# Mamba stage: the product with the old state in halves of the rows, one product for the decays' row sums, one set of eight PSUM banks, and new offsets for the order

## The chip, the cores and the metric

The kernel runs on one core of a Trainium2 chip, in float32 throughout. The time is the device time of one execution in microseconds; the kernel's time is the median over its runs. A core has TensorE (PE, a 128 x 128 array of multipliers that reads its stationary operand by weight loads, PEld, and streams the moving operand past it), VectorE (DVE), ScalarE (ACT), GpSimd (POOL) and SyncE (SP, which here only issues transfers). The results of PE land in PSUM, which holds eight banks of 128 partitions x 512 floats.

## The reference

The input x is an image batch of 2 x 256 x 48 x 48. Layer 0 is a local attention (7 x 7) with a convolution branch. Layer 1 treats the image as 2 x 2304 tokens of 256 features: a Mamba block and then eight experts of which each token takes two. What matters here is the Mamba block's scan, with 8 heads of 64 features and a state of 64:

```python
xn = _rmsnorm(x, norm_w, eps)
zxbcdt = jnp.einsum('bld,ed->ble', xn, W_in)          # z, x, B, C, dt
...
dt = jax.nn.softplus(dt + dt_bias)
dA = jnp.exp(dt * -jnp.exp(A_log))
def step(state, inp):
    dA_t, dt_t, B_t, C_t, x_t = inp
    state = state * dA_t[:, :, None, None] + (dt_t[:, :, None] * x_t)[..., None] * B_t[:, None, None, :]
    y = jnp.einsum('bhpn,bn->bhp', state, C_t)
    return (state, y)
...
y = jnp.moveaxis(ys, 0, 1) + Dp[None, None, :, None] * xs
y = _rmsnorm(y * jax.nn.silu(z), gnorm_w, 1e-05)
return x + jnp.einsum('ble,de->bld', y, W_out)
```

Behind it stand a layer norm, the gating (`xf @ Wg`, the two largest of eight) and the experts (`gelu(xf @ W1[e]) @ W2[e]`, weighted and summed).

## The kernel before

**Three stages.** Layer 0 runs to about 321 us of the span, the Mamba block from there to about 789 us, and the experts to the end at 1294 us. In the last fifth of the Mamba stage PE also works on the first three tiles of one expert ("early" tiles, lines 1805 and 1821), chosen once 24 of the 36 chunks have been gated.

**The scan in chunks.** The 4608 tokens are cut into 36 chunks of 128 (`chunk`, number c), of which three (NJ) make a block of 384 (TB; number k). 18 chunks belong to each image, so two chunks (`fresh`) start from no state and 34 start from the state that the chunk before left. Instead of one step per token, a chunk is computed by products of matrices:

- `pst` (line 1371) forms what the chunk adds to the state: the turned B times the decayed inputs xw. The state is a tile of 128 x 256: heads 0 to 3 on partitions 0 to 63, heads 4 to 7 on partitions 64 to 127, with the 64 state dimensions along the partitions of each half. This product writes its two halves of PE's columns and is marked `mode="tiled"`. POOL multiplies the old state by the chunk's decay (`decayed`, L1397), and DVE adds the two (`state`, L1420).
- `ps` (`from_state`, L1390) is the old state's part of the output: state times C, for all 128 tokens. It makes four matmuls, one for every 128 of the 512 features, with 128 columns of the state as the stationary operand. Since the partitions hold two groups of heads, each matmul takes all 128 rows and the moving operand cz is a tile [128, 2, 384] that holds C twice: in part 0 on the upper 64 partitions with zeros below, in part 1 the other way round. The zeros are written once; two transfers per block (`ct`) copy C in from the tile bc, which has B on partitions 0 to 63 and C on 64 to 127. The result fills one PSUM bank; DVE multiplies it by the tokens' decays rd (`yi`, L1410, one instruction of 128 x 512), and POOL adds that to y (`yb`, L1425).
- `py` (L1433) is the part from within the chunk: eight matmuls into halves of the columns (`mode="tiled"`), of xd and a matrix mt of 128 x 8 x 128 that ACT (`al`, `mt`, L1345 and L1359) and DVE (`mm`, L1353) make from the sums of the decays.
- y goes through `ya` (DVE, L1441), `yz` (POOL, L1443), `sq` (ACT), `sm` (POOL, L1458), `ss` (PE, L1461), `rs` (DVE), `rg` (POOL, L1497), and the product with W_out, `out` (PE, L1451), whose result is added into the residual.

POOL's part of a chunk stands in the lines xw (L1317), dx (L1332), `decayed`, `yb`, `yz`, `sm`, `rg`, and then in the scatters of the gating.

**The decays of a block.** `decays_of` holds `su`, the sums along the chunk, and `er` (`starts`, L1220): for each of the three chunks one matmul with the 8 columns of a as the stationary operand and a triangle of ones as the moving one, so that the results lie as [8 heads, 3 x 128 tokens]. ACT copies them out of the bank twice, once with an exponential, into the tile `from` [8, 2, 384]; the transfer `spread` lays them out in memory as (kind, chunk, head, token), from where `rd` and `row` read them back, spread over partitions.

**Gating.** The chunks are gated in seven groups (6, 6, 6, 6, 6, 4, 2). A group begins when its last chunk's residual is done, forms counts on PE (`g6`, L1609), and ends in two indirect transfers per chunk that POOL issues (`put`, L1679), which scatter the rows to the experts' table. The experts can start when the last of them have landed.

**What sets the order.** Within the Mamba stage all of this is laid out by a list planner (`Flow`). Every operation has an engine, a cost in ns, needs, and slots that it takes and gives back (`room`: six PSUM banks named bank, two named zbank for the projections of the gates z, two cz, three bc, and so on). An operation's rank is its due time (its chunk's number times `PACE1`, 16387 ns), less the rest of its own chain, less an offset per kind of operation (`LEAD1`, 95 numbers). The planner plays the engines' times by these costs; of the operations that are ready and have their slots it emits the one with the lowest rank, with a surcharge where PE would change its mode. The order that it emits is PE's, DVE's, ACT's and SP's order in the program, instruction by instruction, and POOL's is held by explicit order edges. The costs and offsets exist only in the planning: on the chip an instruction starts when its engine has come to it and the tiles it reads and writes are free.

Of the kernel before, what the change touches and what calls it, by code (L numbers as in the profile page):

```python
# [31 lines left out]
F32 = mybir.dt.float32  # L32
# [196 lines left out]
class Kernel:  # L229
# [688 lines left out]
    def mamba(self, ctx):  # L918

        nc = self.nc
        self.ps = self.pool("ps", 1, space=bass.MemoryType.PSUM)
        self.used_banks = ["zbank0", "zbank1"]

        room = dict(bank=6, zbank=2, cvbank=2, t=3, xn=2, xc=2, bc=3, cz=2, z=2, btt=2, xd=3, xw=2,
                    mt=4, yi=1, y=4, sq=2, state=3, rd=2, u2=2, ex=1, ext=1, ehid=2, ey=2)
        self.begin_flow(self.pool("m", 1, ctx), room, self.PACE1, self.LEAD1)
        zeros = self.pool("cz", 1, ctx)
        self.cz = [zeros.tile([P, 2, TB], F32, name=f"cz{i}") for i in range(room["cz"])]  # L930
        for t in self.cz:
            nc.gpsimd.memset(t, 0.0)
        for k in range(B * NBLK):
            self.norms(k)
            self.project_block(k)
            self.decays_of(k)
            for c in range(k * NJ, (k + 1) * NJ):
                self.chunk(c)
        first = 0
        for g, n in enumerate(GROUPS):  # L940
            self.gate(g, first, n)
            first += n
        self.adds = {}
        self.early_expert(sum(GROUPS[: EARLY + 1]))
        for i in range(NEARLY):
            self.early_tile(i, sum(GROUPS[: EARLY + 1]))
        self.run_flow()
# [3 lines left out]
        "al": -290978, "begin": 28518, "btt": 903929, "ct": -258969, "cum": 138318, "cv": 4160,  # L951
        "decayed": 600184, "dg": 29752, "dt": 100727, "dx": -4156, "ea": -277213, "ebegin":
        -102059, "ed": -105474, "efetch": 1438, "eg": 26883, "eown": 41250, "eplan": -216891,
        "eput": -260074, "er": 287202, "es": -882262, "et": -610518, "etoken": -82312, "eu":
        -375317, "ew": 321735, "eweight": -249839, "ex": -22495, "ext": 45975, "from": 77621,
        "g10": -530705, "g5": 86017, "g6": 266930, "g8": 619114, "g9": -284332, "ge": -53696,
        "gm": -98648, "gmrs": 207272, "grs": 157083, "gsm": -121187, "gsw": -603090, "gw":
        -597259, "head": -444384, "kap": 244339, "keep": -167944, "lg": -74165, "mm": 175579,
        "mo": -45640, "mrs": 201963, "msw": -491777, "mt": -64622, "n2": -327525, "nt": 132852,
        "number": -110107, "out": -69798, "pg": -24798, "place": 60192, "ps": 382782, "pst":  # L960
        95326, "put": -322183, "py": 88837, "rd": 122406, "rg": -214014, "row": 58828, "rs":
        216632, "rs1": -164526, "s0": 477684, "s4": 611494, "s5": 133846, "scores": -252255,
        "silu": -226005, "silub": 88047, "silux": 101715, "sm": 481060, "spread": -243362, "sq":
        -69048, "sr": -36881, "ss": -35615, "st": -60640, "state": -249719, "stats": -437860,
        "su": -1199, "tap": 131999, "tb": 14763, "tc": 292305, "tx": 467979, "u2": -251857,
        "xc": 488195, "xd": 18280, "xo": 475933, "xt": 66896, "xw": 407174, "ya": 7940, "yb":
        -85276, "yi": -88374, "yz": -140873, "z": -15500,
# [228 lines left out]
    def decays_of(self, k):  # L1196
# [20 lines left out]
        def starts():  # L1217
            ps = self.bank_for(("er", k))
            for j in range(NJ):
                nc.tensor.matmul(  # L1220
                    ps[:SH, j * P : (j + 1) * P], lhsT=T["a", k][:, j, :], rhs=self.c["le"], start=True, stop=True
                )

        def rows_of(i, func):
            nc.scalar.activation(T["from", k][:, i, :], T["bank", ("er", k)][:SH, :TB], func)

        def spread():
            to = self.decays[k].rearrange("i j s t -> s i j t")
            nc.sync.dma_start(to, T["from", k].rearrange("s i (j t) -> s i j t", j=NJ))
# [8 lines left out]
        op("er", "PE", 660, starts, ("s5", k), takes=[("bank", ("er", k))])  # L1238
        self.chain(k * NJ, ("from", k), [
            ("ACT", 480, lambda: nc.scalar.copy(  # L1240
                self.small_tile("from", k, [SH, 2, TB], bufs=2)[:, 1, :], T["bank", ("er", k)][:SH, :TB])),
            ("ACT", 480, lambda: rows_of(0, AF.Exp)),
# [8 lines left out]
        for i in range(NZ):  # L1251
            at = (k, i)

            def gate(i=i, at=at):
                if i == 0:
                    self.large_tile("z", k, [P, NZ, TB])
                T["zbank", at] = self.next_bank([f"zbank{self.flow.slot['zbank', at]}"], "zbank")
                self.project(
                    T["zbank", at][:, :TB], lambda h: win[:, h, i * P : (i + 1) * P], lambda h: T["xn", k][:, h, 3:]
                )  # L1260

            op(("z", at), "PE", 1300, gate, *rows, ("z", (k, i - 1)) if i else None,
               takes=[("zbank", at)] + ([("z", k)] if i == 0 else []), uses=[("xn", k)])

        taps = [("tap", ((k, m), 2)) for m in range(NM)]
        for i in range(NZ):
# [5 lines left out]
               uses=[("zbank", at)], chain=(("silu", k), i < NZ - 1))  # L1272
# [5 lines left out]
        def ct():  # L1278
            nc.sync.dma_start(self.cz[k % len(self.cz)][:DS, 0, :], T["bc", k][DS:P, :])
            nc.sync.dma_start(self.cz[k % len(self.cz)][DS:, 1, :], T["bc", k][DS:P, :])  # L1280
# [9 lines left out]
    def chunk(self, c):  # L1290
# [56 lines left out]
        def pg():  # L1347
            nc.tensor.matmul(
                self.bank_for(("pg", c))[:, :P], lhsT=T["bc", k][:, cols], rhs=cz[:, 0, cols], start=True, stop=True
            )  # L1350
# [34 lines left out]
        else:  # L1385
            def from_state():
                ps, old = self.bank_for(("ps", c)), T["state", c - 1]
                for m in range(NZ):
                    g, i = divmod(m, 2)
                    nc.tensor.matmul(  # L1390
                        ps[:, m * P : (m + 1) * P], lhsT=old[:, i * P : (i + 1) * P], rhs=cz[:, g, cols],
                        start=True, stop=True,
                    )
# [15 lines left out]
            def yi():  # L1409
                nc.vector.tensor_tensor(  # L1410
                    self.large_tile("yi", c, [P, NZ, P]), self.parts(T["bank", ("ps", c)]), T["rd", c], ALU.mult
                )

            op("rd", "queue", 2800, rd, ("spread", k), takes=[("rd", c)])
            op("ps", "PE", 900, from_state, ("state", c - 1), ("ct", k), ("rd", c), takes=[("bank", ("ps", c))],
               uses=[("state", c - 1)] + ([("cz", k)] if last else []))
# [7 lines left out]
            op("yi", "DVE", 690, yi, ("ps", c), ("rd", c), takes=[("yi", c)], uses=[("bank", ("ps", c)), ("rd", c)])  # L1424
# [941 lines left out]
```

## Time and profile before

| | us |
|---|---|
| median of three runs | 1292.45 (1290.72 to 1294.8) |
| the profiled execution's own time | 1295.8 |
| its span, from the first to the last instruction | 1294.0 |
| stages: layer 0 / Mamba / experts | 321.7 / 467.5 / 504.9 |
| busy in the Mamba stage: PE, DVE, ACT, POOL | 445.8, 356.7, 367.4, 372.7 |
| product with the old state, L1390, 272 records of PE | 36.4 busy |
| yi, L1410, 34 instructions on DVE | 23.3 busy |
| mean granted clock of TensorE | 0.986 |

Lines such as L1390 are lines of the kernel; in the groups of instructions `bank<-cz,state` names the tile written and the tiles read. A float32 matmul stands in the records as two passes, so the 272 records of L1390 are 34 products of four matmuls. The records of neighbouring matmuls overlap, and the sum of their busy times is more than the time that PE gave them; where a price of PE is wanted, it is taken from start to start. PE is busy for 95% of the span, DVE 71%, ACT 61%, POOL 43%; but over the Mamba stage POOL has 372.7 us of 467.5, and its share is uneven.

### The profile page before, as it was taken

To read this page: it belongs to the slowest core of one execution; us is meant where nothing else is said; L and a number is where in the kernel's file an instruction comes from. 1 tells how busy PE (TensorE), PEld (TensorE's weight loads), DVE (VectorE), ACT (ScalarE), POOL (GpSimd) and SP (SyncE) were. 2 spreads that over 40 slices of the span, in tenths; PEclk is the share of its full clock that TensorE was granted. 3 is DMA by queue.
4 is the path that set the end of the run, shared out by engine and by line. 5 is a ranking of instruction groups with operands and counts; after the bars stand their busy time and mean duration, and the time that the engine had idled before them with its cause. 6 is when DMAs were issued, how large, how long until landed. Compare 5 with 4: busy or idle time off the path is not lost. (4 is left out here: it accounts for less than half of the span.)

```text
span 1294.0 us, 23558 instructions
## 1 busy us (share of the span) xinstructions
PE 1232.5 (95%) x8048; PEld 983.4 (76%) x8048; DVE 924.8 (71%) x2425; ACT 792.7 (61%) x1954; POOL 557.6 (43%) x769
## 2 busy tenths in 40 slices
PE   4999999998799999999999997999999999999995
PEld 3566766665567777777777786999999999999994
DVE  5899999999577887879797745555654665566442
ACT  2598978898799888789697552333333333333342
POOL 4411230210357878999889963212121212221220
PEclk9999999999799999999999998999999999999998
DMA  7331322211132234333636238657667667666756
GB/s 283 126 104 41 100 92 76 80 49 41 43 107 89 91 116 120 116 114 120 187 117 186 64 133 278 184 169 254 203 221 236 192 198 228 235 188 199 233 178 208
DMA packets 101658, 194.12 MB, mean 150 GB/s; under 512 B 10635, under 2 KB 82652, under 8 KB 96604
## 3 DMA queue, kind: packets, MB, share of 16 engines
q1 hardware_dynamic: 85020, 168.51, 38.3%
q0 software_dynamic: 14400, 19.74, 7.8%
q10 hardware_dynamic: 2116, 4.33, 1.0%
q8 instruction: 66, 1.08, 0.3%
q14 instruction: 56, 0.46, 0.1%
HBM read 154.24 MB, written 43.23 MB: 153 GB/s over the span
## 5 line engine op out<-in xcount | busy, mean ns | idle before, releaser
L2095 POOL DMA_INDIRECT acc<-ey,token x70 | 108.7, 1552 | 368.5 <-ACT ey L2094 312.1
L2085 PE MATMUL bank<-ext,wt 128*128 128x256 f32 (+1 forms) x1152 | 241.3, 368 | 0.0
L2089 ACT ACTIVATE hid<-bank,bt 128x256 f32<-128x256 f32 (+1 forms) x288 | 132.3, 461 | 170.7 <-PE bank L2085 166.5
L2085 PEld LDWEIGHTS bank<-ext,wt 128*128 128x128 f32 x1152 | 207.0, 190 | 25.0
L681 POOL COPY kp<-kp 128x10 f32<-128x10 f32 (+1 forms) x60 | 24.9, 415 | 179.4 <-DVE kp L674 179.4
L592 DVE SCALAR_TENSOR_TENSOR x<-hid,w2r,x 128x1128 f32<-128x1128 f32 (+3 forms) x72 | 99.9, 1392 | 0.4 <-ACT hid L586 0.2
L2128 PE MATMUL po<-ts,ss 128*128 128x128 f32 x768 | 96.2, 275 | 0.0
L916 PE MATMUL bank<-xn,win 128*128 128x387 f32 x240 | 92.7, 510 | 2.1 <-ACT t L999 2.1
L1129 DVE SCALAR_TENSOR_TENSOR xc<-bank,vec,xc 128x384 f32<-128x384 f32 x144 | 86.6, 610 | 8.4 <-ACT xc L1118 8.1
L2128 PEld LDWEIGHTS po<-ts,ss 128*128 128x128 f32 x768 | 90.9, 192 | 0.0
L1345 ACT ACTIVATE mt<-mt,cum 128x128 f32<-128x128 f32 x288 | 87.8, 393 | 1.7 <-DMA mt<-decays 1.7
L800 ACT ACTIVATE prob<-prob,top 128x308 f32<-128x308 f32 x144 | 78.3, 552 | 16.0 <-DVE top L789 15.6
L1679 POOL DMA_INDIRECT xs<-u,rows x72 | 72.9, 1012 | 17.4 <-issue 14.7
L2132 ACT COPY u<-po 128x128 f32<-128x128 f32 x32 | 8.5, 266 | 114.2 <-PE po L2128 114.2
L2072 DVE TENSOR_TENSOR ss<-hid 128x512 f32<-128x512 f32 x32 | 22.1, 691 | 70.6 <-ACT hid L2089 70.6
L1451 PE MATMUL bank<-wout,y 128*128 128x264 f32 x288 | 72.0, 396 | 0.1
L916 PE MATMUL zbank<-xn,win 128*128 128x384 f32 x192 | 71.2, 492 | 0.5 <-ACT z L1247 0.3
L806 ACT ACTIVATE prob<-prob,rden 128x308 f32<-128x308 f32 x144 | 67.7, 550 | 3.7 <-DVE rden L855 3.7
L582 DVE SCALAR_TENSOR_TENSOR hid<-xp,vec,hid 128x1175 f32<-128x1175 f32 (+1 forms) x48 | 68.4, 1425 | 0.1
L2128 PE MATMUL po<-wt,hid 128*128 128x128 f32 x496 | 65.5, 275 | 0.0
L789 DVE CUSTOM_DVE_ANT_0 prob<-banks,cst 128x308 f32<-128x308 f32 x144 | 61.7, 471 | 3.9 <-PE banks L779 3.6
L916 PEld LDWEIGHTS bank<-xn,win 128*128 128x128 f32 x240 | 42.5, 195 | 24.8 <-issue 3.9
(334 smaller groups left out, 2989.6 us busy)
## 6 DMA issues: line engine op xcount, KB each, us to landing
wt<-in_We SPq DMA_DIRECT2D x36, 2048.0 KB
mt<-decays SPq DMA_DIRECT2D x36, 512.0 KB
ex<-xs SPq DMA_DIRECT2D x36, 265.0 KB
rd<-decays SPq DMA_DIRECT2D x68, 128.0 KB
val<-vtab SPq DMA_DIRECT2D x72, 110.0 KB
bt<-in_We SPq DMA_DIRECT2D x36, 136.0 KB
vraster<-vout SPq DMA_DIRECT2D x18, 256.0 KB
acc<-x SPq DMA_DIRECT2D x36, 128.0 KB
```

The source lines that it names most:

```text
L582: nc.vector.scalar_tensor_tensor(dst, src, w[:, k : k + 1], dst, ALU.mult, ALU.add)
L592: nc.vector.scalar_tensor_tensor(dst, src, w[:, k : k + 1], dst, ALU.mult, ALU.add)
L800: nc.scalar.activation(t, t, AF.Exp, bias=T["top", c][:, a : a + 1], scale=-1.0, accum_out=T["den", c][:, a : a + 1])
L916: self.nc.tensor.matmul(ps, lhsT=lhs(k), rhs=rhs(k), start=k == 0, stop=k == NH - 1)
L1129: nc.vector.scalar_tensor_tensor(out(), T["bank", ("cv", at)][:, i : i + TB], wc[:, i : i + 1], out(), ALU.mult, ALU.add)
L1345: nc.scalar.activation(t, t, AF.Relu, bias=at_s, scale=-1.0)
L1451: nc.tensor.matmul(ps[:, : C + E], lhsT=T["y", c][:, m, :], rhs=self.l1["wout"][:, m, :], start=m == 0, stop=m == NZ - 1,)
L1679: ins = nc.gpsimd.indirect_dma_start(self.xs, bass.IndirectOffsetOnAxis(ap=of("rows")[:, i, q : q + 1], axis=0), T["u2", g][:, i, :], None,)
L2085: nc.tensor.matmul(ps[:, :rows], lhsT=w1[:, k, c * P : (c + 1) * P], rhs=xt[:, k, :], start=k == 0, stop=k == NH - 1,)
L2089: nc.scalar.activation(hid[:, c, :], ps[:, :rows], AF.Gelu, bias=bt[:, c : c + 1])
L2095: put = nc.gpsimd.indirect_dma_start(self.acc, bass.IndirectOffsetOnAxis(ap=token[:, j : j + 1], axis=0), y, None, compute_op=ALU.add)
L2128: nc.tensor.matmul(p[name], lhsT=v[a][:, c], rhs=v[w][:, c], start=c == 0, stop=c == NHC // 2 - 1)
```

## The change

Five edits, all in the Mamba stage.

1. `ps` in halves of the rows: each of its four matmuls takes 64 partitions of the state and the 64 partitions of C that lie on the same rows (cz for the upper half, bc itself for the lower). The two groups of heads write to two banks, ps0 and ps1, of which each uses 256 columns. The operation is marked `mode="rows"` for the planner. `yi` becomes two instructions of 128 x 256, one for each bank.
2. cz is a tile [128, 384] without the second part, so `ct` is one transfer for two, and the tile is half as large to zero. bc is held until the block's last `ps`.
3. `er` is one matmul for the three chunks: its stationary operand is 24 columns of a, the result [24, 128]. The tile `from` becomes [24, 2, 128], and `spread` writes the same layout in memory from it.
4. The PSUM banks: eight named bank, of which the gates' projections take theirs too. zbank remains as a counter (three) with no memory of its own.
5. The planner's costs follow (`ps` 900 to 460, `er` 660 to 224, `yi` 690 to 800, the copies of `from` 480 to 280), and all 95 offsets are replaced, so the order of the whole stage is new.

```diff
-        self.used_banks = ["zbank0", "zbank1"]
+        self.used_banks = []
-        room = dict(bank=6, zbank=2, cvbank=2, t=3, xn=2, xc=2, bc=3, cz=2, z=2, btt=2, xd=3, xw=2,
+        room = dict(bank=8, zbank=3, cvbank=2, t=3, xn=2, xc=2, bc=3, cz=2, z=2, btt=2, xd=3, xw=2,
                     mt=4, yi=1, y=4, sq=2, state=3, rd=2, u2=2, ex=1, ext=1, ehid=2, ey=2)
...
-        self.cz = [zeros.tile([P, 2, TB], F32, name=f"cz{i}") for i in range(room["cz"])]
+        self.cz = [zeros.tile([P, TB], F32, name=f"cz{i}") for i in range(room["cz"])]
...
     LEAD1 = {
-        "al": -290978, "begin": 28518, "btt": 903929, "ct": -258969, "cum": 138318, "cv": 4160,
...
+        "al": -420183, "begin": -574761, "btt": 1202919, "ct": -1073201, "cum": 167539, "cv":
...
         def starts():
-            ps = self.bank_for(("er", k))
-            for j in range(NJ):
-                nc.tensor.matmul(
-                    ps[:SH, j * P : (j + 1) * P], lhsT=T["a", k][:, j, :], rhs=self.c["le"], start=True, stop=True
-                )
+            nc.tensor.matmul(
+                self.bank_for(("er", k))[:n, :P], lhsT=T["a", k].rearrange("p j s -> p (j s)"), rhs=self.c["le"],
+                start=True, stop=True,
+            )
...
         def spread():
-            to = self.decays[k].rearrange("i j s t -> s i j t")
-            nc.sync.dma_start(to, T["from", k].rearrange("s i (j t) -> s i j t", j=NJ))
+            nc.sync.dma_start(self.decays[k].rearrange("i j s t -> (j s) i t"), T["from", k])
...
-                T["zbank", at] = self.next_bank([f"zbank{self.flow.slot['zbank', at]}"], "zbank")
+                T["zbank", at] = self.bank_for(("zb", at))
...
         def ct():
-            nc.sync.dma_start(self.cz[k % len(self.cz)][:DS, 0, :], T["bc", k][DS:P, :])
-            nc.sync.dma_start(self.cz[k % len(self.cz)][DS:, 1, :], T["bc", k][DS:P, :])
+            nc.sync.dma_start(self.cz[k % len(self.cz)][:DS, :], T["bc", k][DS:P, :])
...
             def from_state():
-                ps, old = self.bank_for(("ps", c)), T["state", c - 1]
-                for m in range(NZ):
-                    g, i = divmod(m, 2)
-                    nc.tensor.matmul(
-                        ps[:, m * P : (m + 1) * P], lhsT=old[:, i * P : (i + 1) * P], rhs=cz[:, g, cols],
-                        start=True, stop=True,
-                    )
+                old = T["state", c - 1]
+                to = [self.bank_for((f"ps{g}", c)) for g in range(2)]
+                for i in range(2):
+                    for g, rhs in enumerate((cz[:DS, cols], T["bc", k][DS:, cols])):
+                        nc.tensor.matmul(
+                            to[g][:, i * P : (i + 1) * P], lhsT=old[g * DS : (g + 1) * DS, i * P : (i + 1) * P], rhs=rhs,
+                            start=True, stop=True,
+                        )
...
             def yi():
-                nc.vector.tensor_tensor(
-                    self.large_tile("yi", c, [P, NZ, P]), self.parts(T["bank", ("ps", c)]), T["rd", c], ALU.mult
-                )
+                y = self.large_tile("yi", c, [P, NZ, P])
+                for g in range(2):
+                    part = slice(2 * g, 2 * g + 2)
+                    nc.vector.tensor_tensor(
+                        y[:, part], T["bank", (f"ps{g}", c)][:, :half].rearrange("p (m q) -> p m q", m=2),
+                        T["rd", c][:, part], ALU.mult,
+                    )
...
-            op("ps", "PE", 900, from_state, ("state", c - 1), ("ct", k), ("rd", c), takes=[("bank", ("ps", c))],
-               uses=[("state", c - 1)] + ([("cz", k)] if last else []))
+            banks = [("bank", (f"ps{g}", c)) for g in range(2)]
+            op("ps", "PE", 460, from_state, ("state", c - 1), ("ct", k), ("rd", c), takes=banks, mode="rows",
+               uses=[("state", c - 1)] + ([("cz", k), ("bc", k)] if last else []))
```

In the program's order PE changes the form of its array (full, halves of the columns, halves of the rows) 136 times in this stage before the change and 167 times after it.

## The prediction

> **What bounds the kernel now.** I read the page's slices first (PE at nine tenths from the attention to the end), then the sums by stretch for the Mamba stage (about 321 to 789 us), the only stage that the change touches; the attention before it and the experts after it keep their instructions.
>
> ```profile
> 360.00:460.00 100.00, 99.20 (x628) 70.66 (x627) 81.19 (x227) 89.44 (x216) 71.79 (x99) 1.00 0.31 94
> 460.00:560.00 100.00, 98.43 (x637) 71.20 (x635) 81.32 (x234) 82.37 (x195) 89.89 (x117) 1.00 0.37 112
> 560.00:660.00 100.00, 99.62 (x637) 72.23 (x636) 84.59 (x260) 81.66 (x195) 90.88 (x127) 0.98 0.44 133
> 660.00:740.00 80.00, 78.51 (x517) 59.42 (x516) 65.05 (x174) 62.92 (x148) 74.72 (x102) 1.00 0.45 137
> 740.00:790.00 50.00, 41.51 (x189) 35.15 (x188) 23.41 (x128) 20.06 (x40) 32.39 (x42) 0.93 0.48 137
> ```
>
> The columns are the stretch, its length, busy time of PE, PE's weight loads, DVE, ACT, POOL, then clock and DMA. PE is full until 740. But POOL fills up too: 72 of 100 us, then 90 and more. The waits of POOL between 460 and 740 say how full that is.
>
> ```profile
> POOL xs L1679 <- issue: 9.7, 46, 0.4
> POOL state L1397 <- DVE state L1420: 2.5, 4, 0.9
> POOL kap L1041 <- DVE lg L1476: 2.0, 1, 2.0
> POOL e L1614 <- DVE top L1589: 1.5, 1, 1.5
> ```
>
> The first line is the price of issuing the row scatters (0.96 us and 0.3 of issue each, 1.27 from start to start), not a wait for data. What is left is some 10 us in 280. So POOL starves before 460 and never after, and PE is fed by it: two engines bound this stage.
>
> The timeline gives the true price of a matmul, since its records overlap: from one group's start to the next one's.
>
> ```profile
> 585.46 1.06 PE L1390 MATMUL bank<-cz,state 128*128 128x128 f32 x8
> 586.36 0.40 PE L1609 MATMUL bank<-cnt,cst 128*128 128x48 f32 x2
> ...
> 105.15 0.80 PE L779 MATMUL banks<-kp,q 64*128 64x308 f32 x4
> 105.88 0.33 PE L831 MATMUL bank<-pt,val 110*64 110x128 f32 x2
> ```
>
> The product with the old state (L1390) takes 586.36-585.46 = 0.90 us: four matmuls of two passes, 0.112 a pass. L779 is the attention's product in row halves: two matmuls, four records, 0.73 us.
>
> The end of the stage, from the timeline:
>
> ```profile
> 740.50 0.53 POOL L1497 TENSOR_TENSOR rg<-ss,half 128x1 f32<-128x1 f32 x1
> ...
> 751.66 0.40 PE L1609 MATMUL bank<-cnt,cst 128*128 128x16 f32 x2 [1.16 <-issue]
> ...
> 775.41 0.96 POOL L1679 DMA_INDIRECT xs<-u,rows  x1 [0.30 <-issue]
> ...
> 783.62 5.70 PE L1821 MATMUL bank<-wt,x 128*128 128x256 f32 x16 [6.64 <-issue]
> 789.15 0.60 PE L902 MATMUL bank<-cst,ex 128*128 128x128 f32 x4
> ```
>
> The last chunk's rg on POOL leads in 11.2 us through the last group's gating to its count (L1609), behind which PE's remaining work stands; PE then has a hole of 6.6 us that no releaser explains, and runs its last 16 passes at half clock (5.70 us for what takes 3.6 elsewhere). L902 is the experts' start; from it to the end of the span are 504.9 us of which PE is full, so the change is worth what L902 moves.
>
> **The change, part by part.**
>
> *Products with the old state.* 34 of them, 8 passes of 0.112 = 0.896 us each. In row halves two matmuls run side by side, so 4 pair passes. In L779, of 0.73 us, entering and leaving the mode take about 0.20 (below), which leaves 0.53 = two pair passes of 0.264, for 308 columns: 0.86 ns a column, as the full array has it (0.112 for 128). So 4 x 0.111 = 0.444. Saving 34 x 0.452 = 15.4 us. The trace has no pair with 128 columns; if pairs did not overlap there the saving would be 0, and 15.4 is the other end. I take 15.4: the weight loads of L779 sum to 288 x 184 ns = 53 us and occupy 23.1, so these overlap too.
>
> *Changes of array mode.* Comparing starts around every change with the same form inside a run, over the trace: going into column halves costs 0.14 us, back from them 0.16, into row halves 0.20, out of them 0.19 to full and 0.15 to columns. PE's order in the built program has 136 changes in this stage now (68 in, 68 out: 20.2 us). The new order has 167: 52+6 into columns, 47 back, 34 into rows, 28 from rows to full: 7.3+0.9+7.4+6.9+5.4 = 27.7 with rounding. Cost 7.5 us.
>
> The Trainium skill's "TensorEngine Tiling (Array Packing)", Tiling Modes, speaks against the change: a change of mode drains the array. This trace agrees, with 0.14 to 0.20 us a change. Its Overview promises up to a factor of two for 64 rows; by that alone the sum below would be 20.6 us, where the rows give 13.1. "TensorE: Matmul & The Clock Gate", LDWEIGHTS, prices a load by columns (128/1.2 = 107 ns) whatever the rows; were a pair's two loads to follow each other, 15.4 would shrink to 1.5 (an estimate from that page). The busy time of L779's loads above is against that.
>
> *Row sums of the decays.* 36 matmuls become 12: 24 x 2 passes x 0.109 (L1220's groups) = 5.2 us off PE. ACT's two copies per block from 8x384 (457 and 469 ns) to 24x128; the nearest rows are 266 (128x128 copy, L2132) and 393 (128x128, L1345), so 0.9 to 4.7 us off ACT, on no path here: ACT has 16 of 100 us free.
>
> *yi.* One 687 ns instruction becomes two of 128x256; L1420 has that shape at 415. 34 x 143 = 4.9 us more DVE at most, half of it if the starts overlap. DVE has 15 to 19 us free in 100, so nothing, unless the PE waits for its next piece (first rival).
>
> *One transfer instead of two into cz, smaller memset, one ring of eight banks.* SP issues 12 fewer. PE's waits for cz are 2.2 us in all; between 0 and 2.2 gain, I take 0, since half the product still needs it. A product now holds two banks; the gate projections draw from the same eight. The order was laid out with these counts, so their price is in the order.
>
> *PE sum:* -15.4 - 5.2 + 7.5 = -13.1 us of work. Priced alike, the whole stage has 429.6 us of PE work in the old order and 416.3 in the new one.
>
> *What POOL lets through.* POOL's work is the same in both. Today it is saturated from chunk 9's xw on (461.0; its work till then by rows 93.4). In the new order, PE's work before chunk 9's turn of x is 108.1 instead of 120.1, but chunk 9's yz becomes the late one: py of chunk 9 ends at 122.5 of PE work, at 461.9 with today's stalls, yz 2.3 later, where POOL has 103.0 behind it. 461.9+2.3-103.0 = 361.2 against 461.0+1.1-93.4 = 368.7: POOL runs 7.5 us ahead. Four more scatters (54 for 50) stand before the last rg, 5.2 us, so rg comes 2.3 us earlier, the last scatter 7.5.
>
> *End of the stage.* 740.5-2.3+11.2 = 749.4 for the last count. Behind it PE has 21.2 us of work instead of 28.2, for more of the early experts' tiles stand ahead of it: -7.0. Sum -2.3 - 7.0 = -9.3 us, with hole and half clock kept. The first fetch of the experts follows the last scatter by 4.5 us; at 773.3 it stays hidden.
>
> The profiled execution took 1295.8 us; 1286.5 by this sum. It lay 3.35 over the median of the runs, 1292.45, so I state 1283.
>
> **Rivals.**
> 1. *Slower: the state's add.* In the new order 13 products with the old state (5 today) have under 1.5 us of PE work between them and the matmul whose result the add (L1420, 415 ns, DVE) puts into that state. For it: DVE also has 4.9 us more, and a 1215 ns product (L1353) may stand ahead. At 1.2 us each, PE loses 15.6, net 15.6-9.3 = +6: 1299. Against: today's five wait hardly at all. It decides from 0.7 us each; behind it queue py, out and all else on PE.
> 2. *PE's saving in full, hole gone.* If POOL can be refilled sooner and the unexplained hole does not come back, the fetch binds: 776.5 instead of 789.1, -12.6; with PE alone -13.1: 1279. For it: nothing names the hole's cause. Against: POOL is full.
> 3. *No change.* POOL's start gains nothing because the new order starves it once more (10 us of idle after 460 today, 26 more before): each us there is lost. 1290 to 1294.
> 4. *The halves do not overlap.* PE sum +2.3, 1295.
>
> **How the numbers follow.** 0.3% is 3.9 us, about what a measurement of this kernel tells from no change. Forecast 0.55 (own range 1279 to 1288), full saving 0.14, no change 0.10, state add 0.16, no overlap 0.05. Faster 0.69; same 0.10 and most of 0.05; slower 0.16 and the rest. The range reaches from the full saving with some of the stalls gone too, 1276, over no change to no overlap, 1296; what lies outside is most of the state add's case.
>
> **What the new profile would show.** The product's group at 0.45 us from start to start plus 0.2 for each change; PE's waits for state or for bank pieces of yi near 0; POOL full from about 453; the last rg near 738, the last count near 749, L902 near 780. Wrong would make it: waits of PE at the product's line, a pair pass near 0.22, POOL waits over 10 us after 460, or another hole.

## The result, and the profile after

The changed kernel takes as long as the kernel before: 1294.34 us median (1290.38 to 1298.54, 12 runs) beside 1294.63 us (1290.0 to 1296.58, 12 runs), ratio 1.0005 with a 95% interval of 0.9989 to 1.0021. Forecast was a gain of 0.7%. The profiled execution has a span of 1294.7 us (1294.0 before), PE busy for 1226.0 us (1232.5), 8000 matmul records (8048) and a mean granted clock of 0.980 (0.986).

The sums by stretch, with the same columns as before (stretch, length, PE, weight loads, DVE, ACT, POOL, clock, DMA):

```profile
360.00:460.00 100.00, 99.06 (x629) 68.84 (x630) 81.50 (x241) 93.50 (x226) 73.84 (x103) 0.97 0.27 86
460.00:560.00 100.00, 99.58 (x655) 70.32 (x654) 86.85 (x255) 88.61 (x215) 91.28 (x119) 1.00 0.36 115
560.00:660.00 100.00, 97.03 (x596) 67.88 (x595) 82.28 (x266) 80.98 (x193) 88.42 (x124) 0.97 0.44 136
660.00:740.00 80.00, 77.09 (x506) 56.38 (x505) 58.42 (x165) 51.15 (x118) 71.73 (x93) 1.00 0.43 130
740.00:790.00 50.00, 39.99 (x169) 33.44 (x168) 23.24 (x128) 19.04 (x38) 32.10 (x42) 0.86 0.49 142
```

PE is as full as before up to 560 and busy for 2.6 and 1.4 us less in the two stretches behind, but the stage is not over sooner. What is new is the clock column: 0.97 in two stretches that had 1.00 and 0.98, and 0.86 for 0.93 at the end.

The product itself, from PE's timeline, does what was forecast:

```profile
568.58 1.04 PE L1436 MATMUL bank<-mt,xd 128*64 128x128 f32 x16
569.55 0.37 PE L1388 MATMUL bank<-cz,state 64*128 64x128 f32 x1
569.56 0.37 PE L1388 MATMUL bank<-bc,state 64*128 64x128 f32 x1
569.77 0.27 PE L1388 MATMUL bank<-cz,state 64*128 64x128 f32 x1
...
569.88 0.27 PE L1388 MATMUL bank<-cz,state 64*128 64x128 f32 x1
...
570.20 1.56 PE L916 MATMUL bank<-xn,win 128*128 128x384 f32 x4
```

The two halves start 7 to 10 ns apart; a pair inside the group takes 0.11 us, the first and the last about 0.21 with their part of the change of mode, and the group 0.65 us for 0.90 before.

The end of the stage, from the timelines of POOL and PE:

```profile
744.17 0.53 POOL L1500 TENSOR_TENSOR rg<-ss,half 128x1 f32<-128x1 f32 x1
...
774.99 0.97 POOL L1682 DMA_INDIRECT xs<-u,rows  x1 [0.30 <-issue]
```

```profile
757.16 0.29 PE L1612 MATMUL bank<-cnt,cst 128*128 128x16 f32 x2
...
783.93 6.70 PE L1824 MATMUL bank<-wt,x 128*128 128x256 f32 x16 [6.42 <-ACT x L1816]
790.47 0.60 PE L902 MATMUL bank<-cst,ex 128*128 128x128 f32 x4
```

The last rg comes 3.7 us later (forecast: 2.3 earlier), the last row scatter 0.4 us earlier (forecast: 7.5), the last count 5.5 us later, and L902, the experts' start, at 790.47 for 789.15. The hole ahead of the last 16 passes is there again, and ends almost where it ended before (783.9 for 783.6).

### The profile page after: what moved, and what is told of

Same layout as the page of the kernel before. It is cut to its first block, busy times and chain, and to the rows that moved or that the text cites. A ratio compares the mean times of both kernels' runs of the same rounds, so it can differ in the third digit from the quotient of the medians.

```text
span 1294.7 us, 23428 instructions
## 1 busy us (share of the span) xinstructions
PE 1226.0 (95%) x8000; PEld 970.5 (75%) x8000; DVE 923.8 (71%) x2459; ACT 789.0 (61%) x1955; POOL 556.9 (43%) x769
## 3 DMA queue, kind: packets, MB, share of 16 engines
q1 hardware_dynamic: 84108, 167.33, 37.9%
## 5 line engine op out<-in xcount | busy, mean ns | idle before, releaser
L916 PE MATMUL bank<-xn,win 128*128 128x387 f32 (+1 forms) x432 | 163.8, 514 | 3.2 <-DVE y L1444 1.6
L916 PEld LDWEIGHTS bank<-xn,win 128*128 128x128 f32 x432 | 79.0, 196 | 49.1 <-issue 6.7
L1129 DVE SCALAR_TENSOR_TENSOR xc<-bank,vec,xc 128x384 f32<-128x384 f32 x144 | 86.4, 609 | 13.5 <-ACT xc L1118 12.6
L813 PEld LDWEIGHTS banks<-cst,prob 128*110 128x110 f32 (+1 forms) x432 | 47.5, 129 | 17.2 <-issue 6.9
```

The source lines that it names most:

```text
L916: self.nc.tensor.matmul(ps, lhsT=lhs(k), rhs=rhs(k), start=k == 0, stop=k == NH - 1)
L1129: nc.vector.scalar_tensor_tensor(out(), T["bank", ("cv", at)][:, i : i + TB], wc[:, i : i + 1], out(), ALU.mult, ALU.add)
```

## The experiments

All ran beside runs of the kernel before on the same chip, and ratios are to those. There were five occasions, each on a chip of its own and apart from the recorded comparison; on three of them the changed kernel itself was run again. Of each edit the main lines are shown, shortened where `...` stands.

**First occasion: parts of the change undone.** The product over all 128 rows in the changed kernel's order (`a_fullrows`):

```diff
-                    for g, rhs in enumerate((cz[:DS, cols], T["bc", k][DS:, cols])):
-                        nc.tensor.matmul(to[g][...], lhsT=old[g * DS : (g + 1) * DS, ...], rhs=rhs, ...)
+                    for g in range(2):
+                        nc.tensor.matmul(to[g][...], lhsT=old[:, ...], rhs=cz[:, g, cols], ...)
```

> The changed kernel in its own order, with the product with the old state again over all 128 rows (the zero-padded cz, two transfers, still two banks); nothing else is undone. By the prices from the traces the halves save 34 x (0.90 - 0.44) = 15.4 us of passes and pay about 13 us for 34 entries into and exits from row halves, of which 2.6 us would be paid for column halves anyway: so PE's work should grow by about 5 us. Theory 1 (PE's work is what counts): 5 us slower than the changed kernel. Theory 2 (the saved work is given back by idle time behind POOL): within 1.5 us of it, PE's idle time in the Mamba stage smaller by about 4 us. Theory 3 (the clock falls to half behind a window of 3.41 us in which less than about 0.37 of the time streams columns; in the changed kernel's trace every window under 0.37 was followed by half clock and none above 0.38): the window at 441.8 rises from 0.36 to about 0.5, so no half clock at 445, which gives 1.7 us back.

Measured: 0.9981 (0.9971 to 0.9990), 1288.15 us, mean clock 0.985. PE's work by start-to-start prices is 5.3 us more than the changed kernel's, as priced. No half clock was left between 364 and 776 us, as Theory 3 says.

Row sums in three matmuls again (`a_er3`):

```diff
-            nc.tensor.matmul(self.bank_for(("er", k))[:n, :P], lhsT=T["a", k].rearrange("p j s -> p (j s)"), ...)
+            for j in range(NJ):
+                nc.tensor.matmul(ps[:SH, j * P : (j + 1) * P], lhsT=T["a", k][:, j, :], ...)
```

> The changed kernel in its own order, with the decays' row sums again in three matmuls per block, the 8-row copies and the old layout of the transfer. PE's work grows by 24 x 0.22 = 5.2 us, ACT's by 0.9 to 4.7 us. Theory 1 (PE's work counts): 5 us slower than the changed kernel. Theory 2 (given back behind POOL): within 1.5 us, and PE idle less.

Measured: 1.0005 (0.9996 to 1.0014), 1291.17 us; PE's work 4.7 us more than the changed kernel's. The changed kernel was not run on this chip, so the times decide between the first two theories of neither run. The waits speak for Theory 2 in both: up to the last rg PE idles for 15.0 us with full rows and 14.7 with three matmuls, where the changed kernel has 19.1 to 19.8 on the recorded and the second occasion.

The 16-column matmuls widened (`a_pad`):

```diff
-                    ps[:, j * 2 * SH : (j + 1) * 2 * SH], lambda i: T["xn", k][:, i, cols],
-                    lambda i: win[:, i, DI:XBC],
+                    ps[:, j * P : (j + 1) * P], lambda i: T["xn", k][:, i, cols],
+                    lambda i: win[:, i, XBC - P : XBC],
```

> The changed kernel, with the 16-column matmuls for dt and the scores (72 of them, 144 passes of 0.118 us) widened to 128 columns of the same weights, of which the first 112 results are not read. PE's passes should take the same time (0.112 us for 128 columns), so the order and the work stay. Theory 3 (the share of streaming in a window of 3.41 us sets the next window's clock): the windows at 441.8 and 636.4 rise above 0.37, two half-clock windows fewer, 2 to 4 us faster. Rival (only idle time of PE brings half clock): the half clock at 445 and 640 stays, no change in time.

Measured: 0.9963 (0.9949 to 0.9976), 1286.27 us, clock 0.985, and no half clock between 365 and 740 us.

The new code under the old offsets (`a_oldlead`; the planner's LEAD1 alone is exchanged):

> The new code (halves, one product of row sums, eight banks, new costs) with the old offsets in the planner, so the order is another again. Theory 1 (the new offsets are what lost the gain): 5 to 10 us faster than both. Theory 2 (the gain is given back in any order, since POOL and the end of the stage hold): within 4 us of both kernels.

Measured: 1.0228 (1.0214 to 1.0242), 1320.4 us. Both readings fall. PE's work up to the last rg is even less (384 us), but PE waits 34 us for others instead of 15, and rg comes at 751.5. The old offsets do not suit the new code; that leaves open what still better ones would give.

**Second occasion: the two kernels again, and both faster edits together.** All four profiles of the first occasion lacked the stretch at 773 to 783 us in which PE's hole stands, so both kernels were profiled again.

> The changed kernel unaltered, beside its variants, since in the first profiles of the kernel before and of the changed kernel PE, ACT and DVE all answer late between about 773 and 783 us of the span (PE's hole of 6.6 and 6.4 us), and none of the four variants' profiles has that stretch. If the late stretch belongs to the kernels, it is there again and L902 starts near 790. If it belongs to that execution, L902 starts near 780 to 782 with the half clock at 445 and 636 kept, and the time stays within 0.2% of the kernel before.

> The kernel before unaltered, for a profile beside those of the variants. If the late stretch belongs to that execution, PE has no hole of 6.6 us at 776 and L902 starts near 781 (789.15 less the hole and what half clock it brought).

Measured: the changed kernel 0.9957 (0.9943 to 0.9972), 1286.98 us beside 1292.8. In neither profile is there a hole ahead of the last 16 passes. L902 and what it waits for in the kernel before (POOL's last scatter, then PE):

```profile
774.75 0.96 POOL L1679 DMA_INDIRECT xs<-u,rows  x1 [0.30 <-issue]
...
775.23 3.62 PE L1821 MATMUL bank<-wt,x 128*128 128x256 f32 x16
781.90 0.92 PE L902 MATMUL bank<-cst,ex 128*128 128x128 f32 x4 [3.05 <-issue]
```

and in the changed kernel:

```profile
771.34 0.97 POOL L1682 DMA_INDIRECT xs<-u,rows  x1 [0.30 <-issue]
...
771.84 3.62 PE L1824 MATMUL bank<-wt,x 128*128 128x256 f32 x16
778.19 1.09 PE L902 MATMUL bank<-cst,ex 128*128 128x128 f32 x4 [2.74 <-DMA ex<-xs]
```

PE is through with its own work 3 us before L902 in both, and waits for the fetch of the first expert's rows (the profile names it in the changed kernel alone). L902 stands 7.2 and 6.9 us behind the start of the last scatter. So scatters set the end of the stage here: L902 gains 3.7 us, 3.4 of them at the last scatter.

> The changed kernel in its own order with both edits that made it faster by themselves: the product over all 128 rows, and the 16-column matmuls widened to 128 columns. If both act through the half clock in the middle of the stage, they do not add: 1286 to 1288 on a chip where the kernel before takes 1290.5. If they act apart, 1283 to 1285. No window under 0.37 between 365 and 740 us, so no half clock there.

Measured: 0.9960 (0.9947 to 0.9973), 1287.22 us, clock 0.986. This is no less than widening alone had on the first chip (0.9963), so the two do not add, as the first case says, and the changed kernel beside it has no more (0.9957). One half-clock stretch of 3.4 us was left, at 707.6, which was not expected.

Full rows and three matmuls, that is the old work in the new order with eight banks (`a_full_er3`):

> The changed kernel's order with the work of the kernel before: full rows and three matmuls for the row sums. It leaves of the change only the order and the eight banks. By PE's work it has 5 us more than the full-row variant, 10 more than the changed kernel. Theory 1 (PE's work counts): 1293. Theory 2 (the new order is what gains, the two edits of the work are worth little or less than nothing): 1288 to 1290.

Measured: 1.0007 (0.9996 to 1.0018), 1294.11 us. Against the changed kernel beside it this is 7.1 us more for 10 us more of PE's work: on this occasion PE's work does count, and the order with its eight banks gains nothing alone. The last rg shows how: it comes 3.8 us later than the changed kernel's, for 9.4 us more of work ahead of it and 5.2 less of waiting.

**Third occasion: POOL relieved.**

> The changed kernel unaltered once more, beside the next three. On one occasion it took as long as the kernel before (1.0005), on another 0.43% less. If the late stretch at 773 to 783 us is what took the gain on the first occasion, then a profile without it goes with a ratio of about 0.996 and one with it with about 1.000.

Measured: 1.0020 (1.0009 to 1.0030), 1294.9 us beside 1292.66; the stretch is back (PE's hole is 7.7 us), and its clock over 12 runs is 0.981 on average, the kernel before's 0.987.

POOL's add of yi over a quarter of the features, in both kernels:

```diff
-               lambda: nc.gpsimd.tensor_add(T["y", c], T["y", c], T["yi", c])
+               lambda: nc.gpsimd.tensor_add(T["y", c][:, :1], T["y", c][:, :1], T["yi", c][:, :1])
```

> The changed kernel with POOL's add of yi over one of four pieces of 128 features instead of four (three quarters of the old state's part of the output are left out): about 0.95 x 34 = 32 us less on POOL, nothing else changed and the same order. Theory A (POOL sets the end of the stage through the last scatter: L902 came 7 us behind it in both kernels on a quiet chip): the last scatter comes early, PE becomes the bound; its work, half clock and the waits of the stage's start leave L902 at about 766, 12 us earlier, 1275. Theory B (PE's own chain sets the end): within 2 us of the changed kernel.

> The kernel before with the same part of POOL's add left out. Theory A: PE's work of 426 and 11 us of waits, changes and half clock leave L902 at about 775, 7 us earlier than before, 1285; the difference of the two kernels is then PE's, 9 to 12 us, where with the whole add it was POOL's, 3.4 to 5.6 us. Theory B: no change.

Measured: 0.9978 (0.9965 to 0.9990) for the changed kernel, 5.5 us under the whole one beside it; 1.0000 (0.9987 to 1.0012) for the kernel before. The add takes 0.46 us for 1.27, so POOL has 28 us less to do and not 32; its idle time over the stage grows by 26 us in the changed kernel, and its last rg comes 1.4 us earlier (739.3 for 740.7). Neither theory has the size: 5.5 us lie between the 12 of Theory A and the 2 of Theory B, and the two profiled executions differ by only 0.8. Though POOL is busy for 90% behind 460 us, its load is not, by these two profiles, what holds the last rg for most of the time.

The decay of the state on DVE (`a_dvedec`):

```diff
-                nc.gpsimd.tensor_tensor(
+                nc.vector.tensor_tensor(
...
-            op("decayed", "POOL", 620, decayed, ...
+            op("decayed", "DVE", 420, decayed, ...
```

> The changed kernel with the decay of the old state on DVE instead of POOL (34 instructions of 0.61 us on POOL become 34 of about 0.42 us on DVE), all of the computation kept; the planner lays out another order with it. If POOL sets the end, up to 20 us of POOL's work less bring the last scatter forward and L902 to 768 to 774, 1277 to 1283. If DVE, then at over 90% from 460 to 660, starves PE instead (or the offsets, which were not made for this, lay out a worse order), no gain or a loss.

Measured: 1.0061 (1.0045 to 1.0076), 1300.5 us, the last rg at 745.1: the second case; which of its two reasons holds was not separated.

**Fourth occasion: the open terms beside the changed kernel.**

> The changed kernel unaltered, beside the next three: 0.9957 of the kernel before where the late stretch is absent, 1.0005 to 1.002 where it is there; granted clock 0.981 to 0.984.

> The full-row product in the changed kernel's order again, now beside the changed kernel. By PE's work (price and changes) it has 5 to 6 us more; by the clock (0.9853 against about 0.982) it loses some 4 us less. If the halves gain, it is 2 to 5 us slower than the changed kernel; if their clock eats them, within 1.5 us or faster.

> The widened 16-column matmuls in the changed kernel again, beside it. If the share of streaming sets the clock: clock 0.985 against 0.981 to 0.984, 2 to 5 us faster than the changed kernel. If only idle time does: the same time and clock.

Measured: the changed kernel 1.0016 (1.0002 to 1.0030), clock 0.980; full rows 1.0008 (0.9996 to 1.0019), clock 0.984; widened 0.9988 (0.9980 to 0.9997), clock 0.985; the kernel before 0.987. The halves save 5.3 us of PE's work and gain nothing that can be told (the second case: half clock up to the last rg is 15.0 us in the changed kernel and 8.6 with full rows, the waiting alike); the widening saves no work and gains 0.28%.

The four scatters behind the last row scatter left out (`a_noacc`):

```diff
             def put(j=j):
+                if i < NEARLY - 1:
+                    return
                 ins = pool.indirect_dma_start(self.acc, ...)
```

> The changed kernel without the four scatters with which POOL adds the first two early tiles into the sums (their part of the output is left out); they stand directly behind the last row scatter. If they make the late stretch, PE's hole ahead of its last 16 passes goes and L902 starts 5 to 8 us earlier where the changed kernel beside it shows the stretch, and the time falls by as much. If the row scatters or the occasion make it, no change beyond the 0 to 1 us of POOL's time.

Measured: 0.9955 (0.9939 to 0.9970), 1286.05 us, 0.6% under the changed kernel beside it. PE's hole in the changed kernel on this occasion:

```profile
772.17 1.89 PE L1808 MATMUL bank<-x,wt 128*128 128x256 f32 x8
782.46 6.17 PE L1824 MATMUL bank<-wt,x 128*128 128x256 f32 x16 [8.39 <-ACT x L1816]
788.46 0.60 PE L902 MATMUL bank<-cst,ex 128*128 128x128 f32 x4
```

and without the four scatters:

```profile
770.71 1.89 PE L1808 MATMUL bank<-x,wt 128*128 128x256 f32 x8
774.75 5.41 PE L1824 MATMUL bank<-wt,x 128*128 128x256 f32 x16 [2.14 <-ACT x L1816]
779.99 0.60 PE L902 MATMUL bank<-cst,ex 128*128 128x128 f32 x4
```

6.2 us of the hole go with them. L902 comes 8.5 us earlier, but 2.1 of these lie ahead of the stretch already (the last row scatter starts at 771.2 for 773.4); from the last row scatter to L902 it is 8.8 us for 15.1.

**A fifth chip: PE's wait at the start filled, and the widening in the kernel before.**

```diff
+                if at == (0, NJ - 1):
+                    spare = self.next_bank(["bank7"], "bank")
+                    for _ in range(26):
+                        nc.tensor.matmul(spare[:, :P], lhsT=self.ident, rhs=self.c["le"], start=True, stop=True)
```

> The changed kernel with the widened 16-column matmuls and 26 matmuls of constants (128 columns, results not read, some 5.7 us) in PE's wait of 6.2 us at the start of the stage. If low streaming brings half clock, the 6.8 to 13.7 us of half clock from 326 us on go, which cost 2.8 to 5.3 us of PE; PE also waits 2.7 us for DVE at 355, so 1 to 4 us of that arrive at the last rg: 0.994 to 0.996 of the kernel before without the late stretch, 0.996 to 0.998 with it. If PE's wait there is what counts and not its clock, no gain against the widened variant (0.9963 without, 0.9988 with the late stretch).

> The kernel before with the same 16-column matmuls widened. Its clock is 0.987 already, and its first profile has one half-clock window in mid-stage (640.9, behind a window of 0.32 that holds twelve of these matmuls), its second none. If the share of streaming decides, at most 1.7 us faster, 0.9987 to 1.0; the gain of the widening in the changed kernel (0.28%) is then specific to its order and its halves. If widening helps for another reason, 0.997 here too.

Measured: 0.9984 (0.9975 to 0.9994), clock 0.986, and 0.9986 (0.9974 to 0.9997), clock 0.990 where the kernel before has 0.9865. Neither profile has the late stretch. Beside widening alone on another chip without it (0.9963), filling the wait gained nothing; the two were not run on one chip. Half clock still came at 331.5 (6.8 us) and 362.2 (3.4 us). Widening gains at the edge of what can be told in the kernel before too.

## Why the prediction was wrong

**What was right.** *PE's sum.* Forecast -13.1 us of work; by the prices, with changes of mode, the stage went from 436.9 to 424.6 us in the recorded profiles and from 437.3 to 424.9 on the second occasion: -12.3 and -12.4. A pair takes 0.11 us, and its two weight loads start 10 ns apart and take 0.19 us each, so they overlap too. The estimate that the prediction works out from the LDWEIGHTS section of the Trainium skill's "TensorE: Matmul & The Clock Gate", for two loads that follow each other, does not hold here. Undoing the halves gives back 5.3 us and undoing the row sums 4.7 (forecast 5.2). *PE's work behind the end.* Behind the last rg it falls from 37.9 to 31.2 us, 6.7 (forecast 7.0 behind the last count). *The state's add* (rival 1): no wait of PE for the state of 0.3 us or more is in the list of waits; that rival is out. *The fetch* (rival 2): L902 was to be bound at 776.5 when the hole goes, and starts at 776.4 to 779.8 in six profiles of the changed order without the hole (784.3 in the seventh, which has all of the old work). But the kernel before has it at 781.9 without the hole, so this is no gain of 12.6 us.

**What failed** are the steps "What POOL lets through" and "End of the stage". Up to the last rg, PE's time from 319.5 us on divides like this (work by the prices; half clock, what matmuls in half-clock stretches took beyond their price; the remainder is waiting):

| profile | work | half clock | waiting | last rg | last scatter | L902 |
|---|---|---|---|---|---|---|
| before | 399.0 | 6.9 | 15.1 | 740.5 | 775.4 | 789.2 |
| changed | 393.4 | 11.5 | 19.8 | 744.2 | 775.0 | 790.5 |
| before, second occasion | 398.9 | 5.8 | 14.5 | 738.7 | 774.7 | 781.9 |
| changed, second occasion | 393.7 | 8.6 | 19.1 | 740.9 | 771.3 | 778.2 |

1. *"POOL runs 7.5 us ahead ... so rg comes 2.3 us earlier."* Each term of this was mis-sized. Chunk 9's xw does start at 452.3 for 461.0, 8.7 us ahead, but POOL has done 5.3 us less work by then. What counts is its idle time from 321.7 us to chunk 9's yz, which the step calls the late one: it fell from 55.5 to 52.8 us (55.8 to 53.5 on the second occasion), 2.7 and 2.3 instead of 7.5. The extra work ahead of the last rg is 2.0 and 2.6 us instead of 5.2. And behind that yz POOL waits 4.4 and 1.8 us more, 1.2 of it for issuing four more scatters, which the step put at nothing. Together the last rg is 3.7 and 2.2 us later. Seen from PE, only 5.2 to 5.6 of its 12.4 us lie ahead of the last rg; half clock takes back 2.8 to 4.6 of these and waiting 4.6 to 4.7. Neither engine's load alone holds the last rg: POOL with 28 us less to do moves it by 1.4 us; PE with 5 us more work (full rows) has it at 739.1 on the first occasion, where PE waits 15.0 us, and 1.2 us later than the changed kernel on the fourth, where half clock takes 8.6 us instead of 15.0. PE's saving ahead of the last rg is given back as waiting or as half clock.
2. *"Behind it PE has 21.2 us of work instead of 28.2: -7.0."* True of the work, and not of the time. Behind the last rg POOL has the scatters still to issue, and PE's remaining work fits beside them. From the last rg to the last scatter it is 34.9 and 36.0 us in the kernel before, 30.5 to 30.8 in the changed one, which has four scatters fewer to issue there; the forecast had these 5.2 us as an aside. From the last scatter to L902 it is 6.8 to 7.3 us in nine of the ten profiles without the late stretch (12.0 in that of the old offsets, whose order is another). So what is worth something behind the last rg is the scatters' number there, not PE's work.
3. *"With hole and half clock kept."* The hole was moved along with PE's work as a fixed length. It is no length of PE's: in eight of the nine profiles with the late stretch and all scatters it ends between 0.3 us ahead of and 0.7 us behind the end of POOL's fourth adding scatter (in the ninth, the decay on DVE, 6.0 ahead), and 6.2 us of it go when these scatters are left out. In the profiles with the late stretch and all scatters, L902 comes 13.7 and 13.8 us behind the last scatter in the old order and 14.2 to 15.5 in the new.

The sum where the stretch is absent: rg +2.2, scatters -5.6, behind them -0.3, so L902 moves by -3.7; the profile's span moved by -4.4 and the median of the runs by -5.8, of which the rest is not accounted for. Where it is there, on the recorded occasion: +3.7, -4.1, +1.7, so +1.3, and nothing in the time. The case of no change (rival 3) came true in the time, but its mechanism, POOL starved once more, only in part: its waits behind chunk 9's yz grew by 1.8 to 4.4 us. On the second occasion they grew too, and the kernel gained; the recorded sum is worse than that one in all three terms, by 1.5, 1.5 and 2.0 us.

Half clock ahead of the last rg is a term that no step had. It shows in every run: over the runs of the second to fourth occasion the kernel before has a mean clock of 0.987, the changed kernel 0.980 to 0.984 (0.982 on the recorded one). 0.005 of 1290 us are 6 us, which is the most that it can cost: part of the half clock lies in PE's holes, where it costs nothing.

Left open: what holds the last rg, if neither engine's load does. Two waits of PE that are new with the change, from the profile's list for 320 to 800 us (total, times, longest):

```profile
PE bank L1305 <- DVE y L1444: 2.0, 2, 1.2
PE bank L916 <- DVE y L1444: 1.6, 1, 1.6
```

PE waits there for a bank that DVE's ya (L1444) gives back, 1.6 us of it ahead of the half clock at 636. That a product now holds two banks is not enough to make them: with full rows it still holds two, in the same order, and the list has

```profile
PE bank L1306 <- DVE y L1445: 0.5, 1, 0.5
```

for the first and nothing for the second. On the fourth occasion they are 1.7 and 0.9 with full rows, 2.0 and 1.6 without, so more decides on them than the work.

**A version that is faster than the kernel before.** The changed kernel with the widened matmuls is under the kernel before on both occasions, 0.9963 and 0.9988, and under the changed kernel on the one where both ran, with intervals that don't meet. Whether it also beats the changed kernel where the late stretch is absent (0.9957) was not tried.

## What to carry to other kernels

Before work taken off a full engine is counted as time, ask at which point the engine is last waited for: here more than half of it lay behind that point, where a queue of scatters on another engine sets the end, and the part ahead of it turned into waiting and half clock. Price the granted clock like an engine: a shorter product and a lot of tiny matmuls can lower the share of time in which TensorE streams, and give back as clock what they save as work. Widening matmuls of few columns, of which twelve took 1.44 us here with 16 columns and 1.53 with 128, costs next to nothing and raises that share. A change of a few microseconds has to be measured on several chips before it is believed.

## What the runs showed of the hardware

**Half clock follows little streaming, not only idleness.** In all 20 profiles the half-clock stretches up to 1250 us last 3.41 us or two, three or four times that, and their starts lie on one grid of 3.41 us per profile. Take the stage from 321 to 790 us on that grid, and give each pass its columns times 0.832 ns, the slope between passes of 384 columns (0.322 us) and of 128 (0.109). Of 2569 windows at full clock, 72 were followed by half clock. Every window in which columns stream for less than 0.36 of the time is among them, and none above 0.39; between the two both occur. In layer 0 the border lies somewhat higher: 19 of 1598 windows from 40 to 319 us were followed, with shares of 0.38 to 0.47, and the lowest that was not has 0.40. In the experts, 800 to 1250 us, no share is under 0.67 and no half clock comes. In the changed kernel (sums by stretch, columns as above):

```profile
438.43:441.84 3.41, 3.41 (x24) 2.29 (x24) 3.41 (x9) 3.41 (x10) 0.39 (x2) 1.00 0.11 32
441.84:445.26 3.42, 3.07 (x32) 2.56 (x29) 3.39 (x17) 3.40 (x6) 3.34 (x5) 1.00 0.44 163
445.26:448.67 3.41, 3.41 (x9) 2.20 (x9) 1.96 (x10) 3.07 (x6) 2.53 (x4) 0.50 0.26 77
448.67:452.08 3.41, 3.41 (x26) 3.10 (x25) 3.17 (x10) 2.89 (x8) 1.04 (x1) 1.00 0.11 32
```

PE counts as busy for 3.07 of 3.42 us, and the next window has a clock of 0.50. What lies in that window, from PE's timeline:

```profile
442.29 1.51 PE L916 MATMUL bank<-win,xn 128*128 128x16 f32 x12
443.73 0.37 PE L1388 MATMUL bank<-cz,state 64*128 64x128 f32 x1
...
445.06 2.78 PE L916 MATMUL bank<-xn,win 128*128 128x384 f32 x4 [0.35 <-ACT z L1245]
```

Twelve passes of 16 columns take 1.44 us and stream 0.16; with a product in row halves between changes of mode and 0.35 us of idle time the share is 0.36 to 0.37, by where in a record the columns are laid. Widened to 128 columns on the fourth occasion, the twelve take 1.53 us and the following matmul, at 444.55, runs at full clock:

```profile
441.79 1.60 PE L916 MATMUL bank<-win,xn 128*128 128x128 f32 x12
...
444.55 1.56 PE L916 MATMUL bank<-xn,win 128*128 128x384 f32 x4 [0.26 <-ACT z L1246]
```

But so does that of the changed kernel beside it:

```profile
445.23 1.56 PE L916 MATMUL bank<-xn,win 128*128 128x384 f32 x4 [0.35 <-ACT z L1245]
```

There the same matmuls lie otherwise on the grid, and the share is 0.39 or more. So a work list near the border gets half clock in some executions and not in others, and one window proves little. What widening does shows over all profiles at the start of the stage: the half clock near 326 us lasts 13.65 us in all fifteen profiles without it, and 6.8 to 10.2 in the five with it (in one of these the wait there is filled too).

The Trainium skill's "TensorE: Matmul & The Clock Gate", Part 1, has the clock fall after an idle window of about 3.4 us. This case agrees with the window's length and not with the idleness: the window at 441.84 is idle for 0.35 us.

**A stretch in which every engine answers late.** On three chips (the recorded one, the third and the fourth occasion) DVE waits up to 1.2 us for its own instructions, and ACT up to about 10 us for matmuls that PE's records show as done, from about 1 to 2 us ahead of the last row scatter until about the end of POOL's four adding scatters; on three other chips (both kernels on one, variants on the others) this is in no profile. In the changed kernel on the fourth occasion, from DVE's timeline:

```profile
773.28 0.15 DVE L1941 CAST x<-x 128x1 int32<-128x1 f32 x1 [1.11 <-DVE x L1967]
...
776.81 0.22 DVE L1916 TENSOR_REDUCE x<-x 128x8 f32<-128x64 f32 x1 [0.90 <-DVE x L1956]
...
781.11 0.22 DVE L1949 TENSOR_SCALAR x<-x 128x8 f32<-128x8 f32 x1 [0.33 <-DVE x L1963]
```

Without the four scatters the last such wait is at 773.3 and the kernel is 0.6% faster, 2.1 us of which the profile has ahead of the stretch. That they prolong the stretch is shown; what begins it, and what differs between the chips, is not.
